# Bias rows on GpSimd's queue, the second batch's tokens and norm moved back, and more warming products at the start of a two-layer cross-attention kernel

## The chip, the cores and the metric

The kernel runs on one core of one Trainium2 chip. The metric is device time in microseconds (us) of one execution, lower is better. The core has five engines with instruction streams of their own: TensorE (PE in the profile, with its weight loads as PEld), VectorE (DVE), ScalarE (ACT), GpSimd (POOL) and SyncE (SP, which here only issues DMAs). They meet at semaphores.

## The reference, cut to what matters

Two transformer layers on 4 sequences of 512 tokens with 320 channels, and a context of 1601 tokens with 192 channels for each sequence; 20 heads of 16 channels; all in float32.

```python
h1 = ln(x, n1);  x = attn(h1, h1,      q1, k1, v1, o1_w, o1_b) + x      # self
h2 = ln(x, n2);  x = attn(h2, context, q2, k2, v2, o2_w, o2_b) + x      # cross
h3 = ln(x, n3);  a, g = split(h3 @ ff_w1 + ff_b1)
x  = (a * gelu(g)) @ ff_w2 + ff_b2 + x                                  # feed-forward
```

## The kernel before, in words

**Units.** Attention is cut into units: one sequence ("batch", b = 0..3) and one group of four heads (g = 0..4). The first units are layer 0, self-attention, batch 0, groups 0, 1, 2, ... (called u0, u1, u2 here). A unit needs its queries and keys (`both`, L791, in two halves called `proj`), the values of its batch (`values`, L920, in parts), the maximum of each score row (products `sps`, L959, reduced on DVE into `nmax`, L974), and then the main loop: for each 128 keys the scores `st` (L1185: two products of query and key, high and low parts, and a third with the negated maxima `nrows`), an exponential on ACT (`pr`, L1195), and the product with the values (`av`, L1211).

**Staging.** Queries and keys leave PSUM by ACT as `low` (L807; for u0 as `high`, L802, with DVE making `low`, L803), are split on POOL into a high and a low part (L708, L709), and are moved by six DMAs of 128 KB into the rows of `kT` and `q` that the four-head products read (`move`, L757). During the start, these alternate between SP's queue (the high parts) and ACT's (the low parts).

**The order at the start is written out by hand** (L1507 to L1547); the main loop that follows is planned by costs and due times (`give`, `steps`, `pace`). By hand, in this order: tokens of batch 0 (L175), the weights q, k, v of layer 0 (L206), two bias rows broadcast over 128 partitions (`brow`, L214), tokens of batch 1; the norm of batch 0 (statistics L533 and L534, an inverse root by integer guess and three Newton steps L497 to L513, `hn` L550, transposes L564, `hT` L568 and L573); five warming products (`wps`, L411); `proj` of u0 and its moves; `proj` of u1; the norm of batch 1 up to `hn` (ten steps); the moves of u1; then four rounds of u0's row maxima with the `proj` halves of u2 and a part of the values between them; the moves of u2; u0's `nrows` (L1024 to L1036); then two rounds of u1's maxima with four parts of the values. The main loop then finishes u1's maxima beside u0's scores: in each round half of the products are scores of the running unit and half are maxima of the next.

**PSUM banks.** Eight banks are handed out in the order of expected release (`bank`, L411 and before). A product that is to write a bank waits for the engine that reads the bank's last content. So a `sps` result that DVE has not reduced yet holds its bank.

**DMA lanes.** The listing of the program's instructions shows that the transfers of SP's and ACT's queues take eight completion semaphores (lanes) in turn, and that an issue waits for the transfer that had its lane before it, eight transfers earlier in the program's order. GpSimd's transfers have lanes of their own.

**Adding the bias.** POOL adds the bias row to the tokens of batch 0 (L579) once the row is there; the splits of u1 stand behind that in POOL's stream.

Of the kernel before, what the change touches and what calls it, by code (L numbers as in the profile page):

```python
# [9 lines left out]
F32 = mybir.dt.float32  # L10
# [14 lines left out]
NQ = N // P  # L25
# [48 lines left out]
def kernel(ctx: ExitStack, tc: tile.TileContext, x, context, ws, out):  # L74
# [16 lines left out]


    nc = tc.nc
    dma = nc.sync.dma_start

    const = ctx.enter_context(tc.tile_pool(name="const", bufs=1))
    wpool = ctx.enter_context(tc.tile_pool(name="weights", bufs=1))
# [36 lines left out]
    room = {"turn": 0, "first": 0}  # L134
# [35 lines left out]
    def load_x(b):  # L170

        src = x[b].rearrange("(c p) d -> p c d", p=P)

        def part(t):
            dma(out=xs[b][:, t], in_=src[:, t])  # L175
            loaded[b] = clock["round"] if t == NQ - 1 else 1 << 30

        return [lambda t=t: part(t) for t in range(NQ)]
# [22 lines left out]
    def now(fs):  # L201
        for f in fs:
            f()
# [136 lines left out]
    units = []  # L340
# [35 lines left out]
    stage = [0] * B  # L376


    start = {"on": True}

# [26 lines left out]
    def warm(n):  # L407

        ps = bank("wps")
        for _ in range(n):  # L410
            nc.tensor.matmul(ps[:, : 4 * P], lhsT=ident, rhs=fill, start=True, stop=True)  # L411
        written(0.86 * n, ps)
        busy("act", 0.0, ps)
# [21 lines left out]
    def run(chain):  # L435
        costs, _, ready, _, f = chains[chain].popleft()
        assert ready(), chain
        f()
        clock["credit"] -= sum(costs)
# [54 lines left out]
    def guess_root(var):  # L494

        a, h, y, z = (two.tile([P, NQ], F32, tag=f"root{i}", name=f"root{i}") for i in range(4))
        nc.vector.tensor_scalar(a, var, EPS, None, ALU.add)  # L497
        nc.vector.tensor_scalar(
            z.bitcast(I32), a.bitcast(I32), 1, None, ALU.logical_shift_right
        )  # L500
        nc.vector.tensor_scalar(y.bitcast(I32), z.bitcast(I32), -1, 0x5F3759DF, ALU.mult, ALU.add)
        eng = nc.vector if start["on"] else nc.gpsimd
        eng.tensor_scalar(h, a, -0.5, None, ALU.mult)  # L503
        return h, y, z

    def better_root(h, y, z):


        eng = nc.vector if start["on"] else nc.gpsimd
        eng.tensor_tensor(z, y, y, ALU.mult)  # L510
        eng.tensor_tensor(z, z, h, ALU.mult)
        eng.tensor_scalar(z, z, 1.5, None, ALU.add)
        eng.tensor_tensor(y, y, z, ALU.mult)  # L513
# [197 lines left out]
    def add_proj(u):  # L711
        chain = "early" if u.early else "proj"
# [3 lines left out]
        first = units[u.i - u.g]  # L716
# [30 lines left out]
        def move(of, pairs, may, gap=0):  # L747

            def f():
                pending[of] -= 1  # L750
                u.moving[of] = clock["round"]
                for to, src in pairs():
                    queue = nc.sync
                    if start["on"]:
                        queue = (nc.sync, nc.scalar)[room["first"] % 2]
                        room["first"] += 1
                    queue.dma_start(out=to.bitcast(F32), in_=src)  # L757
                u.open -= 1
                if not u.open:
                    u.when = -9 if start["on"] else clock["round"]  # L760

            pending[of] += 1
            u.moves[of].append((f, may, gap))
            u.moving[of] = clock["round"]
            if (u.i, of, u) not in movers:
                movers.append((u.i, of, u))
# [245 lines left out]
    def max_reduce(u):  # L1012
        if u.pm is not None:
            nc.vector.tensor_reduce(
                u.nm.rearrange("p (j t) -> p t j", t=NQ), u.pm, AX.X, ALU.max, negate=True
            )
            busy("dve", 0.25)

    def max_end(u):

        parts = two.tile([P, SLOT], F32, tag="parts", name="parts")
        high, low = (parts.rearrange("p (j e t) -> p e j t", e=2, t=NQ)[:, e] for e in range(2))
        of = u.nm.rearrange("p (j t) -> p j t", t=NQ)
        nc.vector.tensor_copy(high.bitcast(F32R), of)  # L1024
        nc.vector.tensor_tensor(low, of, high, ALU.subtract)
        turned = two.tile([P, SLOT], F32, tag="turned", name="turned")

        nc.vector.transpose(turned, parts)
        busy("dve", 0.6)
        slots = u.rows.bitcast(F32).rearrange("(g s) n -> s g n", s=DH)[0].rearrange("g (t r) -> g t r", t=NQ)  # L1030

        def rows():
            for i in range(P // SLOT):
                part = slice(i * SLOT, (i + 1) * SLOT)
                queue = (nc.sync, nc.scalar, nc.gpsimd, nc.sync)[i] if start["on"] else nc.sync
                queue.dma_start(out=slots[:, :, part], in_=turned[part, :])  # L1036

        if u.cross and u.before.cross:
            errands.appendleft((clock["round"] + 1, yes, rows))
        else:  # L1040
            rows()
# [391 lines left out]
    def at_once(v):  # L1433
        chain = "early" if v.early else "proj"
        while not v.keyed:
            if not chains[chain][0][2]():
                for w in attn:
                    for todo in w.moves.values():
                        while todo and todo[0][1]():
                            todo.popleft()[0]()  # L1440
            run(chain)
        for todo in v.moves.values():
            while todo:
                assert todo[0][1]()
                todo.popleft()[0]()
# [61 lines left out]
    take_rooms(0)  # L1507
    now(load_x(0))
    now(load_self(0))
    load_bias(0, 0)  # L1510
    load_bias(0, 1)
    now(load_x(1))

    add_norms(0)
    add_proj(units[0])
    warm(5)
    until(lambda: not chains["proj"], "proj")
    at_once(units[0])
    add_proj(units[1])
    add_values(units[0])  # L1520
    run("proj")
    run("proj")
    for _ in range(2 * NQ + 2):
        run("norm")
    at_once(units[1])
    add_proj(units[2])
    first = units[0]
    first.pairs = max_pairs(first)
    for chain in ("proj", "proj", "values", None):
        round_of(first.pairs[0].popleft() + first.pairs[1].popleft())  # L1530
        if chain:
            run(chain)

    at_once(units[2])
    run("values")
    max_reduce(first)
    max_end(first)
    loads.extend(load_x(2))
    for fs in (load_out(0, "o1_w"), load_x(3), load_cross(0)):
        loads.extend(fs)  # L1540
    second = units[1]
    second.pairs = max_pairs(second)
    for _ in range(2):
        round_of(second.pairs[0].popleft() + second.pairs[1].popleft())
        run("values")
        run("values")
    start["on"] = False  # L1547
    clock["credit"] = 0.0

# [46 lines left out]
```

## Time and profile before

| what | value |
|---|---|
| time, median of 3 runs | 3008.98 us (3008.38 to 3009.68) |
| the profiled execution: its own time | 3006.85 us |
| its span, first to last instruction | 3005.1 us |
| PE busy | 2902.2 us, 97% of the span |
| DVE busy | 2115.8 us, 70% |
| ACT busy | 1921.5 us, 64% |
| POOL busy | 1158.6 us, 39% |
| first `st` product of the main loop | at 42.87 us |
| first `av` product of the main loop | at 50.70 us |

The profile is one execution, with times in us from the span's start. A timeline row gives the start, the length of the run of equal instructions, the engine (with a q, as in SPq, for its sequencer issuing DMAs), the line, output<-input, and in brackets the idle time before it and what ended it. A float32 product shows as two records for one instruction. A row of the view by windows gives for a stretch the busy time of each engine, the TensorE clock that was granted (1.00 is full), the DMA engines' busy share and GB/s.

### The profile page before, as it was taken

The page shows a single profiled execution, that of the slowest core. Times are in us where ns is not written, and L with a number is a line of the kernel's source. Part 1 is how long each engine was busy: PE and PEld are TensorE (multiplying, and loading weights), DVE is VectorE, ACT ScalarE, POOL GpSimd, SP SyncE. Part 2 cuts the span into 40 slices and gives each one's busy share as a digit, 9 for nine tenths or more (in the row PEclk, how much of TensorE's full clock was granted, in tenths as well). Part 3 has the DMA queues.
Part 4 walks back from the last instruction along what each step waited for, and adds up shares of the span by engine and source line. Part 5 has one row for each costly group of instructions (what it writes and reads, how often), then busy time and mean ns, then how long its engine had stood idle before and what let it go on. Part 6 is the DMA issues. An engine that isn't in the chain of part 4 may idle for free.

```text
span 3005.1 us, 84209 instructions
## 1 busy us (share of the span) xinstructions
PE 2902.2 (97%) x35210; PEld 1529.1 (51%) x35210; DVE 2115.8 (70%) x4061; ACT 1921.5 (64%) x3780; POOL 1158.6 (39%) x1257
## 2 busy tenths in 40 slices
PE   8999999999999999999999999999999999999999
PEld 4455554555554555455554555545545545544555
DVE  6877888888888888322257778888888888873221
ACT  3766677877877878511147666788778778784110
POOL 3444344454544444201124443444454444442000
PEclk9999999999999999999999999999999999999999
DMA  4454233132132121300123332221221121213000
GB/s 111 100 129 99 67 79 83 45 90 56 37 93 59 38 57 27 94 6 0 33 52 74 96 97 65 70 55 42 53 60 40 49 61 43 55 22 89 10 11 14
DMA packets 165548, 177.13 MB, mean 59 GB/s; under 512 B 72484, under 2 KB 116272, under 8 KB 165168
## 3 DMA queue, kind: packets, MB, share of 16 engines
q1 hardware_dynamic: 164376, 170.56, 22.5%
q8 instruction: 277, 4.54, 0.6%
q10 hardware_dynamic: 760, 1.18, 0.2%
q14 instruction: 103, 0.84, 0.1%
q0 software_dynamic: 32, 0.00, 0.0%
HBM read 55.76 MB, written 29.36 MB: 28 GB/s over the span
## 4 chain that ended last, share of the span: by engine, by line
PE 58%; DVE 8%; POOL 1%; issue 1%; ACT 0%; DMA 0%; SPq 0%; ACTq 0%; POOLq 0%; DVEq 0%
PE av L1211 14%; PE st L1185 10%; PE fps L1314 9%; PE yps L1371 6%; DVE pm L974 5%; PE sps L959 4%; PE vps L920 3%; PE fps L1328 2%; PE ops L1114 2%; PE kps L856 2%; PE qkps L791 2%; DVE nmax L974 2%; PE qps L832 1%; PE sps L986 1%; PE hps L564 1%
## 5 line engine op out<-in xcount | busy, mean ns | idle before, releaser
L1195 ACT ACTIVATE pr<-st 128x512 f32<-128x512 f32 (+1 forms) x2720 | 1404.8, 605 | 400.7 <-PE st L1185 359.4
L974 DVE TENSOR_REDUCE pm<-sps 128x1 f32<-128x512 f32 x1920 | 1186.9, 681 | 158.1 <-PE sps L959 150.1
L1231 POOL TENSOR_TENSOR o<-o,vo 128x512 f32<-128x512 f32 x576 | 740.3, 1285 | 1185.2 <-ACT vo L1230 1157.1
L959 PE MATMUL sps<-kT,q 32*128 32x512 f32 x4800 | 874.5, 429 | 15.2 <-DMA q<-low 5.6
L1211 PE MATMUL av<-pr,vals 128*32 128x512 f32 (+1 forms) x5440 | 738.2, 607 | 64.1 <-DVE pm L974 11.9
L1185 PE MATMUL st<-q,kT 32*128 32x512 f32 (+1 forms) x5120 | 783.7, 421 | 2.4 <-DVE pm L974 1.6
L1185 PEld LDWEIGHTS st<-q,kT 32*128 32x128 f32 (+1 forms) x5120 | 417.8, 180 | 273.1 <-issue 120.7
L1185 PE MATMUL st<-nrows,ones 32*128 32x512 f32 (+1 forms) x2720 | 539.3, 399 | 5.6 <-DMA nrows<-turned 5.6
L959 PEld LDWEIGHTS sps<-kT,q 32*128 32x128 f32 x4800 | 428.3, 184 | 95.0 <-DVE pm L974 19.2
L974 DVE TENSOR_REDUCE nmax<-sps 128x1 f32<-128x512 f32 x640 | 395.2, 681 | 84.7 <-PE sps L959 81.0
L1230 ACT COPY vo<-av 128x512 f32<-128x512 f32 x576 | 354.1, 615 | 33.8 <-PE av L1211 32.0
L1211 PEld LDWEIGHTS av<-pr,vals 128*32 128x32 f32 (+1 forms) x5440 | 111.7, 108 | 343.0 <-DVE pm L974 196.7
L1339 ACT ACTIVATE gl<-fps,b 128x512 f32<-128x512 f32 x80 | 54.7, 687 | 361.3 <-PE fps L1328 253.3
L1314 PE MATMUL fps<-hT,w 128*128 128x512 f32 x640 | 283.2, 596 | 0.0
L1185 PEld LDWEIGHTS st<-nrows,ones 32*128 32x128 f32 (+1 forms) x2720 | 246.3, 180 | 30.0 <-DMA nrows<-turned 3.9
L1340 DVE SCALAR_TENSOR_TENSOR hid<-fps,b,gl 128x512 f32<-128x512 f32 x80 | 59.7, 748 | 240.7 <-ACT gl L1339 238.5
L1314 PEld LDWEIGHTS fps<-hT,w 128*128 128x128 f32 x640 | 119.0, 190 | 150.4 <-issue 149.0
L1371 PE MATMUL yps<-w,hid 128*128 128x320 f32 x640 | 176.7, 435 | 0.0
L1371 PEld LDWEIGHTS yps<-w,hid 128*128 128x128 f32 x640 | 120.1, 190 | 55.5 <-ACT gl L1339 5.3
L1114 PEld LDWEIGHTS ops<-wo,aT 112*32 112x32 f32 (+1 forms) x3072 | 97.8, 110 | 62.1 <-issue 47.7
L1114 PE MATMUL ops<-wo,aT 112*32 112x160 f32 (+1 forms) x3072 | 124.7, 300 | 0.7 <-POOL aT L1096 0.7
L503 POOL TENSOR_SCALAR root<-root 128x4 f32<-128x4 f32 x22 | 5.0, 226 | 310.8 <-DVE root L497 310.1
(86 smaller groups left out, 2490.0 us busy)
## 6 DMA issues: line engine op xcount, KB each, us to landing
kT<-stages SPq DMA_DIRECT2D x160, 200.2 KB
oway<-o SPq DMA_DIRECT2D x80, 256.0 KB
q<-high SPq DMA_DIRECT2D x160, 64.0 KB
q<-low SPq DMA_DIRECT2D x160, 64.0 KB
kT<-high SPq DMA_DIRECT2D x60, 128.0 KB
q<-high SPq DMA_DIRECT2D x60, 128.0 KB
kT<-low SPq DMA_DIRECT2D x57, 128.0 KB
aT<-oway SPq DMA_DIRECT2D x32, 224.0 KB
```

What stands on the lines that cost most here:

```text
L791: nc.tensor.matmul(ps[f : f + m, :w], lhsT=columns[:, f : f + m], rhs=first.hT[:n, k, at : at + w], start=(k == 0), stop=(k == 2),)
L920: nc.tensor.matmul(ps[f : f + m, :w], lhsT=u.kvT[:n, k, at + f : at + f + m], rhs=wv[:n, k, h0 * DH : h1 * DH], start=(k == 0), stop=(k == ...
L959: nc.tensor.matmul(ps, lhsT=u.q[j * SLOT : (j + 1) * SLOT, e, t * P : (t + 1) * P], rhs=u.kT[j * SLOT : (j + 1) * SLOT, u.k0 + s * 512 : u ...
L974: nc.vector.tensor_reduce(to[:, j : j + 1], ps, AX.X, ALU.max, negate=(ns == 1))
L1114: nc.tensor.matmul(ps[f : f + m, : D // 2], lhsT=aT[:n, k, t * P + f : t * P + f + m], rhs=wo[:n, k, cols], start=(k == 0), stop=(k == 2),)
L1185: nc.tensor.matmul(own[0][:r, :], lhsT=ones[rows, :r] if e == 2 else u.keys(rows, c), rhs=u.rows[rows, :] if e == 2 else u.q[rows, e, :], ...
L1195: nc.scalar.activation(p[:r], own[0][:r], AF.Exp)
L1211: nc.tensor.matmul(ps[j * SLOT : (j + 1) * SLOT, :], lhsT=columns_of[:r, head : head + SLOT], rhs=pr.pop((c, j))[:r, :], start=True, stop= ...
L1230: nc.scalar.copy(vo, ps)
L1231: nc.gpsimd.tensor_tensor(u.o, u.o, vo, ALU.add)
L1314: nc.tensor.matmul(ps, lhsT=w1[:, k, i * FF + c * P : i * FF + (c + 1) * P], rhs=u.hT[:, k, :], start=ahead and k == 0, stop=not ahead and ...
L1371: nc.tensor.matmul(ps[:, :D], lhsT=hid[c][:, t * P : (t + 1) * P], rhs=w2[:, c, :], start=(c == 0), stop=(c == NHC - 1),)
```

## The change

The two bias rows are issued by GpSimd's queue. The tokens of batch 1 are issued on SP after the moves of u0. The norm of batch 1 stands at the end of the hand-written order, after two rounds of u1's maxima, and from its first Newton step on it runs on POOL (the flag `first`). A part of the values and a sixth and seventh warming product stand ahead of and behind the first `proj`s: six before the first transposes, one after the first values. Rounds of maxima and the other pieces are interleaved anew. In the start, `nrows` goes half by SP and half by POOL, no longer by ACT. By the listing of both programs, each engine's instructions from the main loop's first `st` on are of the same kinds in the same order; ahead of that, DVE now has the whole norm of batch 1 between the last reductions of the start and the first of the main loop, and POOL has the Newton steps there, ahead of the split of u3.

```diff
-    dma = nc.sync.dma_start
+    queue = [nc.sync]
+
+    def dma(**tensors):
+        queue[0].dma_start(**tensors)
+
+    def by(engine, fs):
+        queue[0] = engine
+        for f in fs:
+            f()
+        queue[0] = nc.sync
...
-    start = {"on": True}
+    start = {"on": True, "first": True}
...
-        eng = nc.vector if start["on"] else nc.gpsimd
+        eng = nc.vector if start["on"] and start["first"] else nc.gpsimd
         eng.tensor_scalar(h, a, -0.5, None, ALU.mult)
         return h, y, z
     def better_root(h, y, z):
-        eng = nc.vector if start["on"] else nc.gpsimd
+        eng = nc.vector if start["on"] and start["first"] else nc.gpsimd
...
-                queue = (nc.sync, nc.scalar, nc.gpsimd, nc.sync)[i] if start["on"] else nc.sync
-                queue.dma_start(out=slots[:, :, part], in_=turned[part, :])
+                way = (nc.sync, nc.gpsimd)[i % 2] if start["on"] else nc.sync
+                way.dma_start(out=slots[:, :, part], in_=turned[part, :])
...
     now(load_x(0))
     now(load_self(0))
-    load_bias(0, 0)
-    load_bias(0, 1)
-    now(load_x(1))
+    by(nc.gpsimd, [lambda i=i: load_bias(0, i) for i in range(2)])
     add_norms(0)
     add_proj(units[0])
-    warm(5)
+    warm(6)
     until(lambda: not chains["proj"], "proj")
     at_once(units[0])
+    now(load_x(1))
+    start["first"] = False
     add_proj(units[1])
     add_values(units[0])
-    run("proj")
-    run("proj")
-    for _ in range(2 * NQ + 2):
-        run("norm")
-    at_once(units[1])
-    add_proj(units[2])
-    first = units[0]
-    first.pairs = max_pairs(first)
-    for chain in ("proj", "proj", "values", None):
-        round_of(first.pairs[0].popleft() + first.pairs[1].popleft())
-        if chain:
-            run(chain)
-
-    at_once(units[2])
-    run("values")
-    max_reduce(first)
-    max_end(first)
+    first, second = units[:2]
+    first.pairs, second.pairs = max_pairs(first), max_pairs(second)
+    for what in "proj proj values warm max moves1 proj max proj max values max rows values max2 moves2 values values max2 values norm norm norm norm norm norm norm norm norm norm".split():
+        if what == "max":
+            round_of(first.pairs[0].popleft() + first.pairs[1].popleft())
+        elif what == "max2":
+            round_of(second.pairs[0].popleft() + second.pairs[1].popleft())
+        elif what == "moves1":
+            at_once(units[1])
+            add_proj(units[2])
+        elif what == "moves2":
+            at_once(units[2])
+        elif what == "warm":
+            warm(1)
+        elif what == "rows":
+            max_reduce(first)
+            max_end(first)
+        else:
+            run(what)
     loads.extend(load_x(2))
...
-    second = units[1]
-    second.pairs = max_pairs(second)
-    for _ in range(2):
-        round_of(second.pairs[0].popleft() + second.pairs[1].popleft())
-        run("values")
-        run("values")
     start["on"] = False
```

More of the change, by code (lines that the diff above doesn't have):

```diff
@@ L752, in f @@
                 for to, src in pairs():
-                    queue = nc.sync
+                    way = nc.sync
                     if start["on"]:
-                        queue = (nc.sync, nc.scalar)[room["first"] % 2]
+                        way = (nc.sync, nc.scalar)[room["first"] % 2]
                         room["first"] += 1
-                    queue.dma_start(out=to.bitcast(F32), in_=src)
+                    way.dma_start(out=to.bitcast(F32), in_=src)
                 u.open -= 1
```

## The prediction

> **What bounds the kernel now.** I read the page first (how full PE is), then the timeline from 0 to 60 us beside the listing of both programs, then narrow windows for the clock, then the waits of SP's queue.
>
> ```profile
> span 3005.1 us, 84209 instructions
> PE 2902.2 (97%) x35210; PEld 1529.1 (51%) x35210; DVE 2115.8 (70%) x4061; ACT 1921.5 (64%) x3780; POOL 1158.6 (39%) x1257
> ```
>
> PE is busy for 97% of the span, and from the first `st` on each engine keeps its order. So the main loop carries whatever lead or lag it is given to the end; the change can act only in the start. I measure it at the first `av` product:
>
> ```profile
> 12.03 5.44 PE L791 MATMUL qkps<-hT,wqk 112*32 112x256 f32 x96
> 15.43 0.54 SPq L757 DMA_DIRECT2D kT<-high  x1
> 15.96 0.56 ACTq L757 DMA_DIRECT2D kT<-low  x1
> 17.29 1.81 SPq L757 DMA_DIRECT2D q<-high  x2
> 18.08 1.65 ACTq L757 DMA_DIRECT2D q<-low  x2
> 18.65 0.50 DVE L533 BATCH_NORM_STATS2 st<-x 128x6 f32<-128x320 f32 x1 [2.72 <-DMA x<-in_x_dram]
> 21.20 0.17 DVE L497 TENSOR_SCALAR root<-mv 128x4 f32<-128x4 f32 x1
> 23.05 1.45 PE L959 MATMUL sps<-kT,q 32*128 32x512 f32 x8 [5.58 <-DMA q<-low]
> 25.29 1.51 DVE L550 TENSOR_SCALAR hn<-x,mv,root 128x320 f32<-128x320 f32 x4
> 26.72 4.86 DVE L974 TENSOR_REDUCE nmax<-sps 128x1 f32<-128x512 f32 x8
> 32.58 4.87 DVE L974 TENSOR_REDUCE nmax<-sps 128x1 f32<-128x512 f32 x8 [0.99 <-PE sps L959]
> 37.48 0.17 DVE L1024 CAST parts<-nmax 128x16 fp32r<-128x16 f32 x1
> 38.03 2.44 DVE L974 TENSOR_REDUCE nmax<-sps 128x1 f32<-128x512 f32 x4
> 42.87 0.50 PE L1185 MATMUL st<-q,kT 32*128 32x512 f32 x2
> 43.65 1.29 DVE L974 TENSOR_REDUCE nmax<-sps 128x1 f32<-128x512 f32 x2 [0.51 <-PE sps L959]
> 50.70 1.06 PE L1211 MATMUL av<-pr,vals 128*32 128x512 f32 x8
> ```
>
> The reader is to see two things. PE idles 5.58 us, from 17.47 to 23.05, for u0's moves. Then DVE sets the pace: the second batch's norm takes it from 18.65 to 26.72, and 24 reductions at 0.61 us follow almost without a gap. The clock:
>
> ```profile
> 22.25:22.50 0.25, 0.00 (x0) 0.00 (x0) 0.25 (x1) 0.00 (x0) 0.25 (x1) 1.00 0.26 74
> 22.50:22.75 0.25, 0.00 (x0) 0.00 (x0) 0.21 (x2) 0.00 (x0) 0.14 (x1) 0.52 0.87 213
> ...
> 32.50:32.75 0.25, 0.25 (x12) 0.23 (x12) 0.17 (x1) 0.00 (x0) 0.17 (x2) 0.50 0.00 0
> 32.75:33.00 0.25, 0.25 (x16) 0.25 (x12) 0.25 (x1) 0.00 (x0) 0.25 (x1) 1.00 0.00 0
> ```
>
> The granted clock halves 5.03 us into that idle time and stays so for 10.25 us. It costs little, since DVE is the slower one there.
>
> **The change part by part.**
>
> *Bias rows and tokens off the front of SP's queue.*
>
> ```profile
> SPq L757 <- DMA x<-in_x_dram: 1.4, 2, 0.8
> SPq L757 <- DMA brow<-in_L_xattn_o_b_dram: 1.3, 1, 1.3
> ...
> 12.05 2.36 SPq L175 DMA_DIRECT2D x<-in_x_dram  x4
> ```
>
> The issues of the bias rows and, behind them, of the tokens end at 14.41, before u0's first part is ready at 15.43: they cost nothing. What cost time is the lanes: `q` waited for the lanes of `brow` and of the tokens. After the change these lanes belong to weights long landed, so ACT issues its three moves back to back: 15.96 + 3 x 0.55 = 17.6 instead of 19.73. Landing: before, 23.05 - 19.73 = 3.3 us after the last issue. I take that: 20.9. Bounds: 1.9 us, the only landing shown, of 4 KB on GpSimd's queue (below), gives 19.5; 23.05 - 18.08 = 5.0 us after the issue of the first `q<-low` (now 16.5) gives 21.5, and half a microsecond for the tokens that now follow gives 22.0.
>
> The bias rows on GpSimd's queue:
>
> ```profile
> 5.42 1.00 POOL L125 MEMSET nrows<- 128x512 f32 x2
> 38.41 0.77 POOL L1036 DMA_DIRECT2D nrows<-turned  x1 [4.45 <-DVE turned L1028]
> nrows<-turned POOLq DMA_DIRECT2D x1, 4.0 KB, 1.9
> ...
> 10.00:11.00 1.00, 0.90 (x5) 0.43 (x5) 0.78 (x3) 0.00 (x0) 0.00 (x0) 1.00 0.97 212
> 14.00:15.00 1.00, 1.00 (x25) 0.62 (x20) 0.48 (x1) 0.23 (x2) 0.00 (x0) 1.00 1.19 105
> 15.00:16.00 1.00, 1.00 (x27) 0.57 (x23) 0.48 (x1) 0.41 (x1) 0.00 (x0) 1.00 0.61 138
> ```
>
> POOL issues them from 6.4, behind its memsets; two at 0.77 us end at 8.0. Behind them stand only the bias additions, which end long before u1's split (before, at 20.69). But the transfers now meet the weights' (the DMA engines are 97% busy at 10 us). The windows from 14 to 16 us, when `brow` was in flight, show 1.8 us of DMA share. So the weights come 0 to 1.8 us later; PE wants the last of them at 12.9. I take 0.3, nearest to nothing, since PE did not wait then. The Trainium skill ("DMA: Bandwidth & Descriptors", section "Issuing engines are not separate DMA queues") says that all queues share the same 16 DMA engines and that another issuing engine only saves issue time. By that rule the new queue by itself earns nothing and the 1.8 us would count; no run here shows two queues meeting in such a way yet.
>
> *More warming, values early.*
>
> ```profile
> 1.54 6.47 PE L411 MATMUL wps<-fill,ident 128*128 128x512 f32 x10 [1.54 <-POOL scales L114]
> 9.77 2.26 PE L564 MATMUL hps<-ident,hn 128*112 128x128 f32 x12 [1.76 <-DVE hn L550]
> 32.48 0.97 PE L920 MATMUL vps<-wv,hT 112*32 112x128 f32 x24
> ```
>
> The sixth product is two records of 0.65: 1.3 us, hidden in 1.76 us of idle. Behind u1's `proj` come values (0.97) and one more (at most 1.3): PE ends at 19.7, before 20.9, hidden too, and beyond 20.9 it would cost the excess. Idle time there shrinks to about 1.2 us; 1.76 us of idle left the clock at 1.00 before, so the fall at 22.5 goes.
>
> *The norm behind the maxima: DVE's chain.* Rounds in the main loop show 43.65 - 42.87 = 0.78 from first product to first reduction: reductions start at 21.7 instead of 26.72. Then 16 x 0.61 = 9.7 (31.4), u0's rows 38.03 - 37.48 = 0.55 (32.0), 8 x 0.61 = 4.9 (36.9). Now the norm: statistics 21.20 - 18.65 = 2.55 (39.4), three steps at 0.2 (40.0), then the root on POOL while DVE waits:
>
> ```profile
> 96.19 0.20 POOL L510 TENSOR_TENSOR root<-root 128x4 f32<-128x4 f32 x1
> 98.20 0.20 POOL L513 TENSOR_TENSOR root<-root,root 128x4 f32<-128x4 f32 x1
> 98.36 1.28 POOL L1231 TENSOR_TENSOR o<-o,vo 128x512 f32<-128x512 f32 x1
> 98.44 1.75 DVE L550 TENSOR_SCALAR hn<-x,mv,root 128x320 f32<-128x320 f32 x2 [0.42 <-POOL root L513]
> ```
>
> Eight steps take 2.21 us, so 13 take 3.6, with 0.04 from engine to engine (98.40 to 98.44) 3.7 (43.7); `hn` 1.51 (45.2). But right behind the root POOL has u3's split, and the last two rows show what happens when a POOL instruction starts beside `hn`: two took 1.75 us instead of 0.76. It is the same at 21.4:
>
> ```profile
> 21.38 1.26 POOL L709 TENSOR_TENSOR low<-low,high 128x512 f32<-128x512 f32 x1
> 21.41 1.26 DVE L498 TENSOR_SCALAR root<-root 128x4 int32<-128x4 int32 x1
> ```
>
> So `hn` loses between nothing and the whole split, 1.26 us for the subtraction and an estimated half of that for the cast, 1.9 us; I take 1.0, as the first of these two rows lost (1.75 - 0.76): `hn` ends at 46.2. Only then come the first main-loop reductions, 2.5 us later than before (43.65), although PE enters the main loop some 8 us earlier. Four results of the first round hold their banks; PE does u3's `proj` and half a round and stops. Queued behind its stopped `sps` are the scores, `av` and u3's second half. Six reductions free the banks up to the first `av` (four of the first round, two of the second), 3.7 us, and the last products take an estimated 0.3 more (a pair of `st` takes 0.50): 4.0, so `av` at 50.2 instead of 50.70: a gain of 0.5. The early start is given back in one wait.
>
> *Half of `nrows` on POOL* instead of ACT: turned at 32.0, two issues of 0.77 and 1.9 to landing, 35.7. PE meets it in the first round, but stops for DVE later anyway: 0.
>
> *The clock in the new wait.* PE stops when the eighth u1 reduction has freed a bank (36.9), `proj` (half of 5.44, 2.7) and half a round (some 0.8, as above) are done: 40.4. It goes on one reduction behind `hn`: 45.8 to 47.7. Idle for 5.4 to 7.3 us; the trace's 5.03 us sufficed for a fall. For about 3.4 us behind the wait DVE still sets the pace; of 10.25 us at half clock that leaves 6.9, whose half is 3.4 us lost. The least is 0, if the clock is back while DVE paces. I take 2.0, nearer the measured end, because the work behind the wait is denser than what kept the clock down before. The Trainium skill ("TensorE: Matmul & The Clock Gate", "What's actually happening") says that one busy window of some 3.4 us gives the full clock back; by that rule this term would be 0, but the rows above show 10.25 us with PE busy nearly throughout.
>
> **Sum.** -0.5 (DVE's chain to the first `av`) + 0.3 (weights) + 2.0 (clock) = +1.8 us on the profiled execution, whose own time is 3006.85 us (1.75 around the span): 3008.65. The median shown is 2.13 above it: **3010.8**, no change by the bound of 0.2%, or 6.0 us, about what a measurement of this kernel can tell.
>
> **The rivals.**
> - *The clock holds in the new wait* (no fall, or back at once): 3010.8 - 2.0 = 3008.8. For it: at the kernel's start 1.76 us of idle did no harm, and the idle estimate lies just beyond 5.03. Chance 0.25.
> - *Slower: the clock falls and stays as long as before.* Place: u0's second main round. From 5 us of idle on it decides; `hn` behind the whole split (1.9 instead of 1.0) makes the idle 7.3. Price: 0.9 more for the split, 3.4 for the clock, 1.8 for weights held up by the bias rows: -0.5 + 0.9 + 1.8 + 3.4 = +5.6; with the moves landing at 22.0, +6.7: 3015.7. Chance 0.10, of which 0.08 beyond 0.2%.
> - *Faster: the norm doesn't hold PE up*, because DVE finds the root done early. Then PE enters the main loop when the rounds are fed, one `nrows` behind 31.4, about 34.4 (31.4 and 0.55, 0.77 and 1.9 for `nrows`) instead of 42.87: 3000.5. Against it: reductions behind `hn` in one stream. Chance 0.04.
> - *The moves don't come earlier*, because tokens and moves share the DMA engines all the same: reductions start 1.1 us later: 3011.9. Chance 0.10.
>
> **How the numbers follow.** The forecast, 3010.8, has 0.51. Its lower ends: landing at 19.5 and no loss in `hn` give -1.4 - 1.0, no fall of the clock -2.0: 3006.4. The upper ends are the slower rival's. I give 3006 to 3015, which leaves out the faster rival and most of the slower one. Faster by over 0.2%: 0.04; slower: 0.08; within: 0.88.
>
> **What would show it.** In the profile of the changed kernel: the first `sps` near 20.9 with an idle below 2 us; reductions from 21.7 on; the first `st` near 34; DVE idle for some 3.7 us before `hn`, released by POOL's root; PE idle for 5 us and more in u0's second round, released by DVE; half clock behind it; the first `av` between 49 and 52. Wrong if PE has no such wait, if the first `av` comes before 47, or if rows later in the main loop differ.

## The result and the profile after

The changed kernel takes 3012.21 us (median of 17 runs, 3008.01 to 3016.32) where the kernel before took 3007.38 us beside it (17 runs, 3004.64 to 3011.23): a ratio of 1.0016, with a 95% interval of 1.0009 to 1.0024. It is slower by 4.8 us, between 2.7 and 7.2. Measured once more (r1 below) the ratio was 1.0022 (1.0013 to 1.0031). So the change lies at the bound of 0.2%, below which the prediction speaks of no change: slower for certain, by about as much as that bound. The profiled execution took 3012.85 us, its span 3011.1.

The page's first lines. PE is busy for 7.3 us more and POOL for 6.2 us more than in the kernel before, and the shares are the same:

```profile
span 3011.1 us, 84223 instructions
PE 2909.5 (97%) x35214; PEld 1530.7 (51%) x35214; DVE 2114.8 (70%) x4049; ACT 1922.3 (64%) x3779; POOL 1164.8 (39%) x1273
```

The start, from the timeline (start, duration, engine, line, operation, and in brackets the idle time ahead with what ended it):

```profile
13.15 5.68 PE L801 MATMUL qkps<-hT,wqk 112*32 112x256 f32 x90 [0.49 <-DMA wqk<-in_L_xattn_k_dram]
15.25 0.47 ACT L812 ACTIVATE high<-qkps,scales 128x256 fp32r<-128x256 f32 x1 [2.40 <-PE qkps L801]
17.52 0.54 ACTq L767 DMA_DIRECT2D kT<-low  x1
18.09 1.25 ACTq L767 DMA_DIRECT2D q<-low  x2
21.07 0.51 PE L969 MATMUL sps<-kT,q 32*128 32x512 f32 x4 [0.31 <-DMA q<-low]
22.73 0.51 PE L969 MATMUL sps<-kT,q 32*128 32x512 f32 x4 [1.15 <-DMA q<-low]
23.26 2.48 DVE L984 TENSOR_REDUCE nmax<-sps 128x1 f32<-128x512 f32 x4 [3.15 <-PE sps L969]
26.36 2.48 DVE L984 TENSOR_REDUCE nmax<-sps 128x1 f32<-128x512 f32 x4 [0.61 <-PE sps L969]
33.92 0.17 DVE L1034 CAST parts<-nmax 128x16 fp32r<-128x16 f32 x1
39.22 0.48 DVE L543 BATCH_NORM_STATS2 st<-x 128x6 f32<-128x320 f32 x1
40.91 4.49 PE L801 MATMUL qkps<-hT,wqk 112*32 112x256 f32 x48
42.01 0.25 POOL L513 TENSOR_SCALAR root<-root 128x4 f32<-128x4 f32 x1 [6.00 <-DVE root L507]
45.59 0.20 POOL L523 TENSOR_TENSOR root<-root,root 128x4 f32<-128x4 f32 x1
45.82 2.80 DVE L560 TENSOR_SCALAR hn<-x,mv,root 128x320 f32<-128x320 f32 x4 [3.50 <-POOL root L523]
46.82 1.27 POOL L719 TENSOR_TENSOR low<-low,high 128x512 f32<-128x512 f32 x1
48.54 7.25 DVE L984 TENSOR_REDUCE nmax<-sps 128x1 f32<-128x512 f32 x12
49.27 1.81 PE L1195 MATMUL st<-q,kT 32*128 32x512 f32 x4 [2.55 <-DVE nmax L984]
53.41 1.94 PE L1221 MATMUL av<-pr,vals 128*32 128x512 f32 x8
60.89 2.07 ACT L1205 ACTIVATE pr<-st 128x512 f32<-128x512 f32 x4
```

The reader is to see four things. First, PE now waits for the k weights, which it didn't before, and u0's first `high` begins at 15.25 instead of 13.70. Second, the reductions do start 3.46 us earlier than before, though only behind the second group of `sps` (22.73), and `parts` stands 3.56 us earlier. Third, DVE then does the norm by itself, waits 3.50 us for POOL's root, and needs 2.80 us for `hn` beside POOL's split, where `hn` took 1.51 us before. Fourth, the first reduction of the main loop comes at 48.54 instead of 43.65, the first `av` at 53.41 instead of 50.70.

The last row of that fence is the first exponential of the third round of the main loop. In the kernel before it is this one:

```profile
55.87 1.58 ACT L1195 ACTIVATE pr<-st 128x512 f32<-128x512 f32 x3
```

I call the distance from 55.87 the **lag** of a run (negative: a lead); it is 5.02 us here, and still 4.99 us at the 65th exponential, where before stands at 110.5 us. The granted clock, in windows (length, busy time of PE, PEld, DVE, ACT, POOL, the clock, the share of DMA, GB/s):

```profile
24.00:24.50 0.50, 0.50 (x11) 0.21 (x4) 0.50 (x2) 0.00 (x0) 0.00 (x0) 0.52 1.06 382
27.00:27.50 0.50, 0.50 (x11) 0.20 (x7) 0.50 (x2) 0.00 (x0) 0.00 (x0) 0.57 0.21 57
...
41.00:41.50 0.50, 0.50 (x8) 0.28 (x12) 0.49 (x2) 0.50 (x2) 0.00 (x0) 0.58 0.00 0
47.75:48.00 0.25, 0.00 (x0) 0.00 (x0) 0.25 (x1) 0.12 (x1) 0.25 (x1) 0.82 0.00 0
58.00:58.25 0.25, 0.25 (x8) 0.14 (x4) 0.00 (x0) 0.25 (x1) 0.00 (x0) 0.70 0.00 0
```

It is halved (called half clock below) from 24.0 to 27.4, from 41.1 to 44.5 and, from within PE's wait for DVE, from 47.9 to 58.15.

### The profile page after: what moved, and what is told of

It is laid out like the page before. It is cut to its first block, busy times and chain, and to the rows that moved or that the text cites. A ratio compares the mean times of both kernels' runs of the same rounds, so it can differ in the third digit from the quotient of the medians.

```text
span 3011.1 us, 84223 instructions
## 1 busy us (share of the span) xinstructions
PE 2909.5 (97%) x35214; PEld 1530.7 (51%) x35214; DVE 2114.8 (70%) x4049; ACT 1922.3 (64%) x3779; POOL 1164.8 (39%) x1273
## 4 chain that ended last, share of the span: by engine, by line
PE 57%; DVE 8%; POOL 1%; issue 1%; ACT 1%; DMA 0%; SPq 0%; POOLq 0%; ACTq 0%; DVEq 0%
PE av L1221 14%; PE st L1195 10%; PE fps L1324 9%; PE yps L1381 6%; DVE pm L984 5%; PE sps L969 4%; PE vps L930 3%; PE fps L1338 2%; PE ops L1124 2%; PE kps L866 2%; PE qkps L801 2%; DVE nmax L984 1%; PE qps L842 1%; PE sps L996 1%; PE hps L574 1%
```

## The experiments

My theory after the result: two parts of the change cost, each by itself. The norm at the end of DVE's chain makes the first rounds of the main loop late, and half clock behind that wait adds to it. The bias rows on GpSimd's queue hold the k weights up, and with them everything up to the norm. The rivals: only one of the two; or the clock alone, whose phase differs between executions.

All kernels in one table. "`high`" is the start of u0's first `high`, "`hn`" the end of the second batch's norm, "`av`" the first `av`, each from one profiled execution; the ratio is to the kernel before, from 10 to 17 runs with 15 to 33 of the kernel before beside them.

| kernel | `high` | `hn` | `av` | lag | ratio (95%) |
|---|---|---|---|---|---|
| before | 13.70 | 26.80 | 50.70 | 0 | 1 |
| changed | 15.25 | 48.62 | 53.41 | +5.02 | 1.0016 (1.0009 to 1.0024) |
| r1: changed, again | 15.46 | 47.78 | 52.58 | +3.99 | 1.0022 (1.0013 to 1.0031) |
| e1: bias on SP | 15.17 | 47.70 | 52.49 | +3.48 | 1.0011 (1.0001 to 1.0020) |
| r3: bias on SP, again | 13.70 | 47.33 | 52.12 | +3.64 | 1.0015 (1.0006 to 1.0024) |
| e2: root on DVE | 15.39 | 45.26 | 50.05 | +1.86 | 1.0004 (0.9995 to 1.0014) |
| e3: norm started behind u0's rows | 14.96 | 42.48 | 49.88 | -0.82 | 1.0006 (0.9996 to 1.0015) |
| e4: four more products in the wait | 15.22 | 47.65 | 51.95 | +1.25 | 1.0007 (0.9998 to 1.0017) |
| e5: e1 and e3 together | 13.70 | 42.53 | 49.85 | -0.85 | 0.9997 (0.9989 to 1.0006) |
| e6: before, bias on GpSimd | 15.63 | 26.22 | 50.81 | +0.10 | 0.9998 (0.9989 to 1.0007) |
| e7: before, tokens late | 13.81 | 28.99 | 52.90 | +2.20 | 1.0010 (0.9999 to 1.0022) |
| e8: norm ahead of the maxima | 13.70 | 38.08 | 50.24 | -0.46 | 0.9994 (0.9985 to 1.0003) |
| e9: e8 and one more product | 13.70 | 35.74 | 47.84 | -2.86 | 1.0004 (0.9994 to 1.0013) |

**e1, the bias rows back on SP's queue.**

```diff
-    by(nc.gpsimd, [lambda i=i: load_bias(0, i) for i in range(2)])
+    load_bias(0, 0)
+    load_bias(0, 1)
```

> The changed kernel, with the two bias rows back on SP's queue, behind the weights; everything else as changed. In the changed kernel the first exponential of the third main round is 5.02 us later than in the kernel before (the lag). Theory (the bias rows on GpSimd's queue hold up the k weights): the first projection runs without its 0.49 us wait for the weights and the gap behind it, u0's high part is ready at about 15.4 us instead of 16.96, every step behind it moves up by 1.5 us, and the lag falls to about 3.5 us; time about 1.5 us below the changed kernel. Rival (the moves of u0 wait for the tokens' transfers anyway, so an earlier projection is lost in the queue): the reductions start at 23.3 us as before and the lag stays at 5.0.

The wait for the k weights was gone, but `high` was late all the same: in this execution the clock was at 0.50 while PE projected.

```profile
12.00:13.00 1.00, 1.00 (x10) 0.40 (x12) 0.44 (x1) 0.64 (x1) 0.00 (x0) 0.50 0.79 245
```

So this profile tells nothing of the weights' share: the reductions start at 23.36, as late as in the changed kernel, and the lag of 3.48, which the theory had forecast, does not come of an earlier projection. The kernel was run again as r3, below.

**e2, the Newton steps on DVE.** The line that sends them to POOL is taken out.

```diff
-    start["first"] = False
```

> The changed kernel, with the Newton steps of the second norm on VectorE instead of GpSimd. Theory (it matters where the norm stands, and only a little who does it): 13 steps at 0.2 us are 2.6 us instead of 3.50 us of waiting, and hn starts about 0.9 us earlier; whether it still meets u3's split decides on up to 1.3 us more; the lag falls from 5.0 to between 2.8 and 4.2 us. Rival (GpSimd is the cause): the lag falls by 3.5 us or more, to 1.5 or less, since the whole wait goes.

```profile
43.75 1.51 DVE L560 TENSOR_SCALAR hn<-x,mv,root 128x320 f32<-128x320 f32 x4
45.18 2.48 DVE L984 TENSOR_REDUCE nmax<-sps 128x1 f32<-128x512 f32 x4
```

`hn` takes 1.51 us again, and DVE has no wait ahead of it: POOL, without the root, starts its split only at 45.83, when `hn` is done. From the first statistics (38.23) to the end of `hn` are 7.03 us; in the changed kernel (39.22 to 48.62) 9.40. That is 2.4 us for the root's place. The lag, 1.86, lies between the ranges of the theory (2.8 to 4.2) and the rival (1.5 or less); it is 2.1 us below r1's and 3.2 below the first profile's.

**e3, the norm started behind u0's rows.** Six of the ten `norm` steps move from the end to right behind `rows`; only `hn` stays at the end.

```diff
-max values max rows values max2 moves2 values values max2 values norm norm norm norm norm norm norm norm norm norm
+max values max rows norm norm norm norm norm norm values max2 moves2 values values max2 values norm norm norm norm
```

> The changed kernel, with the norm's statistics and root right behind u0's rows and ahead of u1's maxima, and only hn at the end: GpSimd's root then runs beside eight reductions. Theory (the wait for GpSimd's root in front of the first reductions of the main loop is what gives the early start back): no wait before hn, the 3.50 us and the 1.3 us lost beside u3's split go, the first main reductions start at about 44 us instead of 48.5, PE has no wait of 2 us in the second round, and the lag falls from 5.0 to between -1 and +1.5 us. Rival (the lag is made by the clock and by the late start of the maxima, the wait only covers it): the lag stays above 3.

```profile
36.93 2.15 PE L930 MATMUL vps<-wv,hT 112*32 112x192 f32 x24 [2.96 <-DVE nmax L984]
49.88 1.07 PE L1221 MATMUL av<-pr,vals 128*32 128x512 f32 x8
...
179.91 0.47 ACT L817 ACTIVATE low<-qkps,scales 128x256 f32<-128x256 f32 x1 [4.24 <-DMA kT<-low]
180.43 0.79 PE L969 MATMUL sps<-kT,q 32*128 32x512 f32 x1 [3.15 <-ACT low L817]
```

POOL's root now lies beside DVE's eight reductions, `hn` follows without a wait, and the lag of 4 to 5 us becomes a lead of 0.82: the order of DVE's chain is what made the start late. PE's wait for DVE is not gone: it stands ahead of the main loop (2.96 us at 36.93), with half clock from 35.95 to 46.2, and the `av` comes 0.82 us earlier than before all the same. But the time does not fall below that of the kernel before. The last two rows show where this execution loses its lead: ACT waits for the moves of a split at 180 us, PE waits for ACT, and around it the clock is at 0.50 (179.3 to 186.1). At the 165th exponential (212.1 us before) the lead is a lag of 1.28.

**e4, PE's wait filled.** Four warming products ahead of u0's second main round.

```diff
+                if u.i == 0 and c == 1:
+                    warm(4)
                 round_of(products)
```

> The changed kernel, with four warming products (1.7 us at full clock, no part of the result) ahead of the second main round, where TensorE waits for VectorE. Theory (the wait drops the clock, and half clock behind it costs more than the wait): the granted clock no longer halves at 48 us, the first av stays where it is within 0.7 us (VectorE sets it), and the lag in the third round falls from 5.0 to about 2.7 us. Rival (the lag is the wait for VectorE alone): the lag stays at 5.0 or grows by the products' 1.7 us.

```profile
48.00:49.00 1.00, 0.94 (x11) 0.40 (x8) 1.00 (x3) 0.00 (x0) 0.00 (x0) 1.00 0.00 0
51.00:52.00 1.00, 0.91 (x12) 0.34 (x13) 1.00 (x3) 0.73 (x2) 0.00 (x0) 1.00 0.00 0
```

The clock holds where it fell in the changed kernel. The lag at the first `av` is 1.25, and at the third round still 1.25: nothing is added behind the `av`. (I had expected a lag of 2.7 and the `av` within 0.7 us of where it was; it stands 0.63 us ahead of r1's and 1.46 ahead of the first profile's.) In the changed kernel 2.71 at the `av` became 5.02, in r1 1.88 became 3.99, in e1, r3 and e2, where the clock falls there too, 1.69 to 2.51 us were added. So the clock's part behind the `av` is some 2 us, and the wait for DVE with what lies ahead of it is the rest. That the wait makes the clock fall is not shown: e4 is one execution, and in e2 the clock fell at 48.4 though PE had been busy for 3.17 of the 3.4 us ahead, with no wait above 0.2.

**e5, e1 and e3 together.** Both edits.

> The changed kernel with two edits: the bias rows back on SP's queue behind the weights, and the second batch's statistics and root started right behind u0's rows, with only `hn` left at the end. Theory (the loss is the norm at the end of DVE's chain, plus the weights held up by the bias rows; each acts alone): PE does not wait for the k weights, the first part of u0 is ready as in the kernel before when the clock is full, the reductions start by 22.5, the first main-loop reduction stands at 41 to 42 (43.65 before), the lead at the third round's first exponential is 1 to 3 us, and the time is 1 to 3 us below the changed kernel with the norm moved alone: 0 to 2 us above the kernel before, since some 2 us of any lead are lost between 165 and 200 us where ACT waits for moves. Rival (that later loss comes of the two issues that left SP's queue, which shift all later lanes): with the issues back, the lead at 110 us is still there at 210 us and the time is 1 to 3 us below the kernel before. Second rival (only the clock's phase decides): no order in the lags, time as the changed kernel, 4 us above the kernel before.

```profile
13.70 0.47 ACT L812 ACTIVATE high<-qkps,scales 128x256 fp32r<-128x256 f32 x1 [0.86 <-PE qkps L801]
41.02 1.51 DVE L560 TENSOR_SCALAR hn<-x,mv,root 128x320 f32<-128x320 f32 x4
```

The slowdown is gone: 0.9997, though the lead, 0.85, is short of the 1 to 3 us expected. With the changed kernel, e1 and e3 it makes a square of two edits. Mean ratios of the kernels that ran twice are 1.0019 (changed, r1) and 1.0013 (e1, r3). The norm's place is then worth 1.0019 - 1.0006 = 0.0013 with the bias rows on GpSimd's queue and 1.0013 - 0.9997 = 0.0016 without: 3.9 and 4.8 us. The bias rows are worth 1.0019 - 1.0013 = 0.0006 and 1.0006 - 0.9997 = 0.0009: 1.8 and 2.7 us. With half-widths of some 0.0006 for the kernels measured twice and 0.0009 for the others, such a difference is known to about 0.0011: the norm's part stands in both rows of the square, the bias rows' part in neither, and rests on the traces. The rival of the expectation (shifted lanes) falls: with both issues back on SP a lead of 0.85 still became a lag of 0.78 at 212 us. So does the second one (the clock's phase alone): the two profiles of one kernel differ by up to 1.0 us in their lags, and those with the norm moved stand 4.3 to 5.8 us ahead of those without.

**e6, the kernel before with the bias rows on GpSimd's queue.**

```diff
-    load_bias(0, 0)
-    load_bias(0, 1)
+    by(nc.gpsimd, [lambda i=i: load_bias(0, i) for i in range(2)])
```

> The kernel before with one edit: the two bias rows are issued by GpSimd's queue. Theory (two queues share the DMA engines, so the bias rows delay the weights): PE waits 0.3 to 0.5 us for the k weights near 12.6 us, as in the changed kernel, where the kernel before has no such wait; the projection of u0 and u1 ends 0.3 to 1.5 us later; the tokens, issued up to 1.3 us earlier, bring the statistics forward from 18.65 to 17.5 to 18.5, so the lag at the third round is between -1 and +0.5 and the time within 1.5 us of the kernel before. Rival (the queue is harmless and the wait of the changed kernel has another cause): no wait for the k weights, lead of about 1 us kept, time 1 us below. Rival (the late weights cost what they delay): lag of 1.5 us, time 1.5 us above.

```profile
13.14 6.28 PE L800 MATMUL qkps<-hT,wqk 112*32 112x256 f32 x92 [0.16 <-DMA wqk<-in_L_xattn_k_dram]
15.63 0.47 ACT L811 ACTIVATE high<-qkps,scales 128x256 fp32r<-128x256 f32 x1 [2.83 <-PE qkps L800]
17.77 0.48 DVE L542 BATCH_NORM_STATS2 st<-x 128x6 f32<-128x320 f32 x1
```

The weights are late here too (PE gets the k weights at 13.14, as at 13.15 in the changed kernel). `high` begins 1.93 us later, much of it through half clock from 11.6 to 15.0, as in e1. It costs nothing: the statistics, which the tokens set, start 0.88 us earlier, and DVE paces from there. The same delay costs only where PE and the moves set the start, as they do in the changed kernel.

**e7, the kernel before with the tokens behind u0's moves.**

```diff
-    now(load_x(1))
...
     at_once(units[0])
+    now(load_x(1))
```

> The kernel before with one edit: the second batch's tokens are issued behind u0's moves; the norm stands ahead of the maxima as in the kernel before. Theory (the tokens' lanes held the moves up): ACT issues its moves for u0 without the gap of some 1.6 us, the first sps stands at 21 to 22 instead of 23.05, but DVE now waits for the tokens until 23 to 25 and only then does the norm (8.1 us) and the maxima: the first reduction at 31 to 33 instead of 26.72, lag 4 to 6 us at the third round, time 3 to 6 us above the kernel before. It shows that the tokens can't move without the norm. Rival (the transfers themselves, not the lanes, set the moves): first sps at 23 again.

```profile
16.70 1.75 ACTq L757 DMA_DIRECT2D q<-low  x2
20.71 0.63 PE L959 MATMUL sps<-kT,q 32*128 32x512 f32 x4 [3.12 <-DMA q<-low]
21.64 0.49 DVE L533 BATCH_NORM_STATS2 st<-x 128x6 f32<-128x320 f32 x1 [5.60 <-DMA x<-in_x_dram]
```

The lanes do what the prediction said: ACT issues its `q<-low` from 16.70 on instead of 18.08, right behind `kT<-low`, and the first `sps` comes 2.34 us earlier, with nothing else changed. The tokens landed sooner than I expected (21.64, not 23 to 25), so the lag is 2.20 and not 4 to 6, and the time, expected 3 to 6 us above the kernel before, is not clear of it (1.0010).

**e8, the norm ahead of the maxima.** e1, the tokens back at the front, six `norm` steps ahead of the first `max` and four behind `rows`.

```diff
-    by(nc.gpsimd, [lambda i=i: load_bias(0, i) for i in range(2)])
+    load_bias(0, 0)
+    load_bias(0, 1)
+    now(load_x(1))
...
-    now(load_x(1))
...
-proj proj values warm max moves1 proj max proj max values max rows values max2 moves2 values values max2 values norm norm norm norm norm norm norm norm norm norm
+proj proj values warm norm norm norm norm norm norm max moves1 proj max proj max values max rows norm norm norm norm values max2 moves2 values values max2 values
```

> The changed kernel with the bias rows and the tokens back on SP's queue where the kernel before has them, the statistics ahead of u0's maxima (where DVE waits for u0's moves anyway), the root on POOL beside the maxima, and `hn` right behind u0's rows. Theory (DVE's chain sets the start; its idle 18.65 to 23 is where the statistics cost nothing): statistics from 18.7 to 20 on, first sps near 23, first reduction at 23.5 to 24, u0's rows at 33.5 to 34.5, `hn` at 34 to 36 with no wait, the first main-loop reduction at 40 to 41.5 instead of 43.65, a lead of 2 to 3.5 us at the third round, 0 to 2 of which are lost near 165 to 200 us: time 0.5 to 3 us below the kernel before. Rival (PE, not DVE, sets the entry, or the clock falls in a new wait): lag between -0.5 and +3, time equal to the kernel before or up to 3 us above.

```profile
18.47 0.49 DVE L543 BATCH_NORM_STATS2 st<-x 128x6 f32<-128x320 f32 x1
30.90 5.11 DVE L984 TENSOR_REDUCE nmax<-sps 128x1 f32<-128x512 f32 x8 [1.80 <-PE sps L969]
```

The statistics cost nothing where they now lie, but the clock was halved from 22.2 to 39.2 in this execution and DVE waited for `sps` again and again; the lead is 0.46 instead of 2 to 3.5. 0.9994 is the lowest ratio of all, and not to be told from 1.

**e9, e8 with one more warming product** (`warm(2)` instead of `warm(1)`).

> The kernel with the norm ahead of the maxima, and one more warming product behind u1's projection, in PE's wait of some 2 us for u0's moves. Theory (with the norm out of DVE's end the lag is set by half clock in the start, where DVE waits 1 to 2 us at a time for PE): the idle ahead of the first sps shrinks from 2.07 to 0.5 to 1 us; where the clock then stays whole to 25 us and beyond, DVE's waits for sps shrink by 1 to 3 us in all, the first main-loop reduction comes at 38.5 to 40.5 and the time is 1 to 2.5 us below the kernel before. Rival (the clock falls all the same, because PE is busy for less than half of the time while DVE reduces): half clock from 22 to 30 us again, lag within 1 us of that of the kernel with the norm ahead, time equal to it.

```profile
35.65 7.26 DVE L984 TENSOR_REDUCE nmax<-sps 128x1 f32<-128x512 f32 x12
...
178.74 0.79 PE L969 MATMUL sps<-kT,q 32*128 32x512 f32 x1 [3.01 <-ACT low L817]
```

Here the clock was halved only from 23.7 to 27.1 and from 40.75 to 44.2, and the start did what e8 was meant to: a lead of 2.86 us, the first `av` 2.86 us earlier. At 178.74 PE waits as in e3, and at 212 us the lead is 0.56. The ratio is 1.0004, where I had expected 1 to 2.5 us less than before: the best start of all is not a faster kernel.

**r1, the changed kernel again.**

> The changed kernel once more, word for word, for a second profiled execution and a second ratio. Theory (the order of DVE's chain decides, the clock's phase adds to it): the wait of PE for DVE ahead of u0's second main round and `hn` at 2.2 to 2.8 us stand again, `hn` ends between 47.5 and 49, the k weights are waited for again by 0.3 to 0.5 us, and the lag at the third round is 2 to 6 us, other than 5.02 by what the clock does; ratio 1.0005 to 1.0025. Rival (the 5.02 us of the first profile are that execution's own bad luck with the clock): lag below 1.5, ratio within 0.0005 of 1.

```profile
15.46 0.48 ACT L812 ACTIVATE high<-qkps,scales 128x256 fp32r<-128x256 f32 x1 [2.81 <-PE qkps L801]
23.42 9.66 DVE L984 TENSOR_REDUCE nmax<-sps 128x1 f32<-128x512 f32 x16 [3.10 <-PE sps L969]
44.99 2.79 DVE L560 TENSOR_SCALAR hn<-x,mv,root 128x320 f32<-128x320 f32 x4 [3.48 <-POOL root L523]
48.44 1.32 PE L1195 MATMUL st<-q,kT 32*128 32x512 f32 x4 [2.63 <-DVE nmax L984]
```

Each wait stands where it stood. The clock fell at 39.85, not 41.1, and at 50.1, not 47.9, for 6.8 us instead of 10.25, and not at all at 24: its phase belongs to the execution, the waits to the kernel.

**r2, the kernel before again.**

> The kernel before once more, word for word, for a second profiled execution. If the lags of one profile are the kernel's own, it follows the first one to 0.3 us up to 200 us. If the phase of the clock's windows differs from execution to execution, its clock falls at other times than 22.5 and 172.5, its lag at the third round is still below 1 us (DVE paces the start there), and between 165 and 600 us it gains or loses 1 to 3 us: then a lag of that size behind 165 us in any one profile says nothing of an edit.

```profile
20.00:21.00 1.00, 0.00 (x0) 0.00 (x0) 0.90 (x4) 0.00 (x0) 0.92 (x2) 0.79 0.60 201
34.00:35.00 1.00, 1.00 (x14) 0.47 (x16) 1.00 (x3) 0.00 (x0) 0.00 (x0) 0.62 0.93 193
```

The clock fell at 20.6 and at 34.2, not at 22.5, and the lag against the first profile is +0.93 at the third round, -1.15 at the 565th exponential and -2.57 at the last. So of the lags in the table some 1 us is the execution's own, and behind 200 us up to 3.5 us; the medians, not these, decide the time.

**r3, e1 again.**

> The changed kernel with the bias rows back on SP's queue, once more, word for word, since half clock covered the projection in its first profile (u0's first `high` part began at 15.17 us, as late as in the changed kernel, though no wait for the k weights stood ahead of it). Theory (the bias rows on GpSimd's queue hold the k weights up by 1.5 to 1.8 us): with the clock whole at 12 us the first `high` begins at 13.5 to 13.8 as in the kernel before, the first sps at 19.5 to 20.3, `hn` ends at 45.7 to 47, the first `av` stands 1.4 to 1.9 us ahead of the changed kernel's 52.58 to 53.41, and the ratio is 1.0005 to 1.0016. Rival (the weights come late for another reason): the first `high` at 15 or later with the clock whole, and a wait for the k weights.

```profile
13.70 0.47 ACT L812 ACTIVATE high<-qkps,scales 128x256 fp32r<-128x256 f32 x1 [0.86 <-PE qkps L801]
19.50 0.51 PE L969 MATMUL sps<-kT,q 32*128 32x512 f32 x4 [0.32 <-DMA q<-low]
52.12 1.94 PE L1221 MATMUL av<-pr,vals 128*32 128x512 f32 x8
```

With the clock whole, `high` is back at 13.70 to the hundredth and the first `sps` 1.57 us earlier than in the changed kernel: the bias rows on GpSimd's queue are what held the weights up. At the `av` only 0.46 to 1.29 us of it are left, where I had expected 1.4 to 1.9. The clock fell at 22.5 here, and DVE then waited 0.78 us for `sps`.

## Why the prediction was right, and where it was not

The range held, no change by 0.2% held by the median ratio (1.0016; by r1, 1.0022, it would not), and the mechanism did: the earlier start is given back in one wait for DVE. But the price, 1.8 us above the kernel before, was measured as 4.8. That the time forecast, 3010.8, is only 1.4 us off is partly luck: the median that it was built on, 3008.98 from three runs, stands 1.6 us above the 3007.38 of 17 runs. Of the signs named, the wait of DVE for POOL's root (3.50 us), PE's wait for DVE and half clock behind it are there, and the first `av` does not come before 47. But the first `st` came at 36.80 and not near 34, PE's wait was 2.55 us and not 5, and the first `av`, at 53.41 and 52.58, lies outside 49 to 52; and rows later in the main loop do differ (last point below). Two sums were off without weight in the forecast: the faster rival's entry is 34.6, not 34.4, and the terms given for `nrows` land it at 35.4, not 35.7. The terms, for the two profiles of the changed kernel:

- *Lanes and moves: right, with two errors in the first `sps` that cancel.* ACT issues its three moves without a gap (17.52 to 19.34), and the second group of `sps`, the last to wait for `q<-low`, stands 3.4 us behind, where I took 3.3. e7 shows the gap go by itself. The first group needed less and came 1.7 us behind, at 21.07, near the 20.9 forecast although the projection was 1.55 late: that is luck. The first reduction waited for the second group (it begins at 23.26, when that ends) and so stands 2.2 us behind the first `sps`, not 0.78.
- *The weights: sized wrong, and the step that failed.* I took 0.3 us of a bound of 0 to 1.8, "since PE did not wait then". Measured: 15.25 - 13.70 = 1.55, in r1 1.76. PE did not wait before, but the weights had less room than the new transfers took; a row of no wait says nothing of how much room is left. The issue row (160 KB each, and the median time from issue to landing) gives the reason:

```profile
brow<-in_L_xattn_o_b_dram POOLq DMA_DIRECT2D x2, 160.0 KB, 4.8
```

  These transfers were under way for 4.8 us each, from 6.4 and 7.2 on, while the k weights, issued from 7.48 on, moved too. All five profiles with this edit in the changed order show PE's wait for the k weights (0.28 to 0.67 us), and none with the bias rows on SP's queue does. The rule of the Trainium skill that I had weighed against my choice ("DMA: Bandwidth & Descriptors", "Issuing engines are not separate DMA queues") was the better guide: the trace agrees with it, by 1.55 us.
- *DVE's chain: right.* I had forecast reductions from 21.7 and the end of `hn` at 46.2. In r1 the first is 23.42, 1.72 later, all of it the weights; `hn` ends at 47.78, 1.58 later. So the chain between is as predicted to 0.14 us, with the wait for POOL (3.48 for 3.7) and `hn` beside the split (a loss of 1.28 for 1.0). The first profile has 0.77 us more, where DVE waited for `sps` at half clock from 24 to 27.4: I had said that the fall at 22.5 goes; in that execution it only moved, and in r1 there is none before 39.85.
- *From `hn` to the first `av`: short by 0.8.* 4.8 us in both profiles for 4.0.
- *PE's wait: half as long as forecast.* I had PE stop at 40.4 and idle for 5.4 to 7.3 us. It stopped at 46.7 and idled for 2.55, because u3's `proj` began at 40.91, not near 36.9, and then ran at half clock for 4.49 us. In e1, where this `proj` began at 38.56 with the clock whole, the wait was 5.66. The wait's end, which is what counts, came where DVE's chain put it.
- *The clock: right in size, wrong in its condition.* It fell with 2.55 us of idle, where I had asked for 5.03; in r1 it fell only at 50.1, when PE had been at work again since 48.44. 2.0 us expected; 5.02 - 2.71 = 2.31 and 3.99 - 1.88 = 2.11 measured, and none in e4. The rule of the Trainium skill ("TensorE: Matmul & The Clock Gate", "What's actually happening") that one busy window gives the full clock back would have made this term 0. Here half clock lasted 10.25 and 6.8 us, with PE busy for 8.9 and 6.8 of them.
- *Sum at the third round:* for the first profile -0.5 + 1.55 (weights) + 0.77 (DVE at half clock) + 0.10 (what is left of the norm) + 0.79 (to the `av`) + 2.31 (clock) = 5.02. The rival that came nearest is the slower one, whose +5.6 took the weights at 1.8.
- *Lag and lead are carried to the end: wrong in general.* The four leads, -0.82, -0.85, -0.46 and -2.86 at the third round, were +1.28, +0.78, +0.80 and -0.56 at 212 us. But lags lose as much there. Between the 65th exponential (110.5 us) and the 165th (212.1 us), e2, e4, r1 and r3 fall back by 1.1 to 2.4 us, e3, e5, e8 and e9 by 1.2 to 2.3, and e6, with no lag, by 1.35. All of these have PE's wait for ACT, here in e2:

```profile
183.64 0.49 PE L969 MATMUL sps<-kT,q 32*128 32x512 f32 x1 [3.18 <-ACT low L817]
```

  It is 1.8 to 3.4 us long in these nine, 0.92 in the changed kernel, which lost 0.6 us, and below 0.8 in e1, e7, r2 and the first profile of before, which all the others are compared with; these lost 0.2 us at most. e1 and r3 are one kernel, and only r3 has the wait. So the place takes from lags and leads alike, and it can come in one execution of a kernel and not in another. Both profiles of before are without it. What decides whether it comes was not tried, and stays open.

None of the versions beats the kernel before by what can be measured; the intervals of e5, e8 and e9 all hold 1, as those of the changed kernel do not.

## What to carry to other kernels

A wait that isn't there in the profile says that something arrives in time, not with how much to spare: before moving a transfer to another queue, look at when it will be in flight and what else is, and price the whole overlap. Work that is put off to the end of an engine's chain comes due just ahead of the next stage; give its slow part (here the root on POOL) something to lie beside, as e3 did. And where a clock's phase differs between executions, take a second profile of the same kernel before a lag of 1 or 2 us is put down to an edit.

## What the runs showed of the hardware

The granted clock fell without any long idle time: in the changed kernel at 24.0, behind waits of 0.31 and 1.15 us, and at 41.1, behind 1.06 and 0.41 us; PE was busy for 1.94 of the 3.4 us ahead of either fall, and in e2 (48.4) and e9 (40.75) for 3.17 and 3.30 of them. I had taken 5 us of idle as what it needs; what it does need stays open. The stretches at half clock lasted 3.4, 6.8 or 10.25 us, or 13.65 in e7 and 17.1 in e8, about a multiple of 3.4 us each. The same kernel showed them at other places in each execution (22.5 us in the first profile of before, 20.6 and 34.2 in the second). The Trainium skill ("TensorE: Matmul & The Clock Gate", "What's actually happening") states a free-running window of about 3.4 us, with which these lengths agree; that it takes an idle window for a fall, as the same section has it, they do not show.
